# A graph layer on one core: where the third pair's rows, one block of x, one weight and two loads of destinations stand at the hand-over to the edges

## The chip, the core and the metric

One Trainium2 chip; the program runs on one of its cores, in one launch. The metric is the device time of an execution in microseconds (us). Engines are named as in the profile: PE (TensorE matmuls), PEld (its weight loads), DVE (VectorE), ACT (ScalarE), POOL (GpSimd), SP (SyncE, which issues DMAs here); ACTq and SPq are the sequencers of ACT and SP where they issue DMAs.

## The reference

Node features x (6250 x 128), and 100,000 edges (src, dst), sorted by dst. All float32. Cut to what matters:

```python
msg_in   = concatenate([x[src], x[dst]], -1)          # 100000 x 256
h        = relu(msg_in @ Wm1 + bm1)                   # 256
h        = relu(h @ Wm2 + bm2)                        # 256
messages = h @ Wm3 + bm3                              # 128
agg      = segment_sum(messages, dst) / clip(count, 1)
node_in  = concatenate([x, agg], -1)
upd      = relu(node_in @ Wn1 + bn1) @ Wn2 + bn2
out      = layernorm(x + (x + upd))
```

## The kernel before, in words

**Tables.** `x @ Wm1` is computed once a node and not once an edge. Table A (`atab`) holds `x` times the upper half of Wm1, table B (`btab`) `x` times the lower half, split into three bf16 terms. Thirteen blocks of four 128-node tiles are transposed (L307), multiplied (L258) and stored to DRAM by SP (L267 for A, L276 for B). B's rows are put together on their way to DRAM in seven slots of 768 columns (`spare`, `SLOT`, `SLOTS`) in the third plane of `acc`. `acc` is the array of sums, 128 partitions x 3 planes x nodes: two planes are the 256 hidden values, the third counts edges, and the third plane is not summed into until the edges begin. In this stage SP also loads the weights (`weights`, L186), and ACT issues the loads of the edges' destinations for the first three pairs (`destinations`, L375, called at L432; the tiles are `db`, three buffers).

**x's part.** `x_part` (L347) multiplies a block of x by the upper half of Wn1 in two PSUM tiles, adds the bias on ACT or DVE and writes the result over `xT` and `x_sb`. It is four passes of PE a block (two products, each recorded as two passes). Four blocks go between B's last blocks, six behind them (the loop at L447), block 9 (`X_FIRST`) after the first pair's first layer (L687), two more at the end. A small product `pb3` (L449 to L452) gives the bias `b23`.

**Edges.** Edges are taken in groups of 512, and groups in pairs: 98 pairs. For each pair:

- `destinations` loads dst, broadcast over partitions, in two DMAs from ACT (L384);
- `fetch` (L484) gathers A's rows by src with eight indirect DMAs from POOL (L492), and reads B's rows in windows of 22 nodes with eight DMAs (L498). They are SP's, but of the first pair, whose second group's four are ACT's. Both land in `rows`, which has two buffers;
- `hot` (L507) makes on DVE the one-hot matrices that spread B's windows to edges (L516) and edges to nodes (L519);
- `first_layer` (L527) transposes A's rows into PSUM (`ph`, 32 matmuls, L533), adds B's rows by one-hot matmuls (16, L540), and evicts with relu on ACT (four ACTIVATEs, L546). `ph` has one buffer, so the next pair's transposes wait for these evictions;
- `second_layer` (L551) multiplies by Wm2 (32 passes, L555) and evicts on DVE (L557, four);
- `sums` (L559) adds up the edges of a window of nodes (L565), `part_of` copies (L573), `turned` transposes (L584), `add_up` adds the windows into `acc` (L594, DVE).

The steps of neighbouring pairs are interleaved: while pair p is in its first layer, pair p-1 is in its second, p-2 in `sums`, p-3 in `add_up`, and POOL and SP fetch pair p+1. Before the first `add_up`, B's slots in the count plane are cleared on DVE (`clear`, L641): three in step 0, two each after the second layer of steps 1 and 2.

**Order.** The order on PE, ACT and POOL is as written (`manual_schedule`); DVE's is as written from B's last blocks on; SP's is as written while the tables are stored. Each DMA of SP and ACT is given one of eight completion counters in turn, in the program's order, and its issue waits until the DMA that had the counter before has landed. Each engine's queue is in order, so what waits holds up all behind it.

After the edges, the node stage computes the update and the layernorm; the change does not touch it.

Of the kernel before, what the change touches and what calls it, by code (L numbers as in the profile page):

```python
# [9 lines left out]
F32 = mybir.dt.float32  # L10
# [17 lines left out]
def kernel(  # L28
# [121 lines left out]
    with tc.tile_pool(name="prep", bufs=1) as prep, tc.tile_pool(  # L150
# [36 lines left out]
        def weights(block):  # L187
            for t in (wu1, w3, w2):
                nc.vector.tensor_copy(t[:, 0, :1], xT[:, block * 4 * P:block * 4 * P + 1])
            nc.gpsimd.dma_start(nb2[:, 0, :], bm2.rearrange("(o h) -> o h", o=1).to_broadcast([P, H]))  # L190
            nc.sync.dma_start(wu1, wn1.rearrange("(k p) h -> p k h", p=P))
            nc.sync.dma_start(w3, wm3.rearrange("(k p) h -> p k h", p=P))
            nc.sync.dma_start(w2, wm2.rearrange("(k p) h -> p k h", p=P))

# [180 lines left out]
        def destinations(g, ng, dst_row):  # L375

            db = ld.tile([P, 2, 2 * P], I32, name="db", bufs=3)
            if isinstance(g, int) and g < 6:

                nc.vector.tensor_copy(db[:, 0, :1], srcT[:, 0, :1])  # L380
            for h in range(2):
                edges = dst_row[:, ds(g * GE, ng * GE)].rearrange("o (s e) -> o s e", s=ng)
                edges = edges[:, :, h * 2 * P:(h + 1) * 2 * P]
                nc.scalar.dma_start(db[h * NQ:(h + 1) * NQ, :ng, :], edges.to_broadcast([NQ, ng, 2 * P]))  # L384
            return [db[:, k, :] for k in range(ng)]
# [20 lines left out]
        for i in range(BLOCKS):  # L406
# [22 lines left out]
            if i >= BEHIND:  # L429
                b_block(i - BEHIND)  # L430
            if BLOCKS - 3 <= i:
                early.append(destinations(2 * len(early), 2, dst_row))  # L432
        assert not blank
        behind = list(X_BEHIND)
        with tc.manual_schedule(engines={ENG.DVE}):
            for n, j in enumerate(range(BLOCKS - BEHIND, BLOCKS)):
                if n < 4:
                    whole(x_part(behind.pop(0), bank_pb, (nc.scalar, (nc.scalar, nc.vector)[n % 2])))
                b_block(j)
                b_stores()  # L440
            b_terms()
            b_stores()
        stores.close()


        turns.enter_context(tc.manual_schedule(engines={ENG.DVE}))
        for n, b in enumerate(behind):  # L447
            whole(x_part(b, bank_pb, (nc.vector if n >= len(behind) - 2 else nc.scalar, nc.vector)))
        pb3 = pp.tile([P, 1], F32, name="pb3", tag="pp")  # L449
        for c in range(HC):  # L450
            nc.tensor.matmul(pb3, w3[:, c, :], b2[:, c:c + 1], start=(c == 0), stop=(c == HC - 1))
        nc.vector.tensor_add(b23, b3, pb3)  # L452

# [10 lines left out]
    with edge, tc.tile_pool(name="wk", bufs=2) as wk, tc.tile_pool(  # L464
# [18 lines left out]

        def fetch(groups, queues):  # L484


            rows = ld.tile([P, 2, (GT + 1) * H], F32, name="rows", bufs=2)
            got = []
# [37 lines left out]

        def first_layer(got, ohts, nts):  # L527
            ph = p1.tile([P, 2, 2, HC, 2 * P], F32, name="ph")
            for i, ((ag, bw), nt) in enumerate(zip(got, nts)):
                for c in range(HC):  # L530
                    for u in range(GT):
                        for h in range(nt // 2):
                            nc.tensor.matmul(ph[:, i, h, c, u * NQ:(u + 1) * NQ], ag[halves[h], u, c * P:(c + 1) * P],  # L533
                                             ident[halves[h], halves[h]], is_transpose=True,
                                             start=(c == 0 and u == 0), stop=False, skip_group_check=True)
            for i, ((ag, bw), nt) in enumerate(zip(got, nts)):
                for c in range(HC):
# [5 lines left out]
            for i in reversed(range(len(nts))):  # L543
                nh = nts[i] // 2
                for c in range(HC):
                    nc.scalar.activation(h1[:, i, c, :nh * 2 * P].rearrange("p (h e) -> p h e", h=nh),  # L546
                                         ph[:, i, :nh, c, :], AF.Relu, bias=b1[:, c:c + 1])
            return h1
# [89 lines left out]

        slots = list(range(SLOTS))

# [6 lines left out]
        for i in range(NP + 4):  # L647
# [7 lines left out]
            if i < NP:  # L655
                dbs = early.pop(0) if early else destinations(2 * i, min(2, NGF - 2 * i), dst_row)
                if 2 * i + 1 == NGF:
# [3 lines left out]
                          for g, (_, eng) in zip((2 * i, 2 * i + 1), queues)]  # L661
                got = fetch([(srcT[:, 2 * i + k, :], firsts[k]) for k in range(2)], [q for q, _ in queues])
                st[i] = dict(nts=NTS[2 * i:2 * i + 2], got=got, dbs=dbs)
# [17 lines left out]
            if p + 1 < NP:  # L681
                make_hot(p + 1)
            if p == 0:
                clear(3)
            if p < NP:
                s = st[p]
                s["h1"] = first_layer(s.pop("got"), s.pop("ohts"), s["nts"])  # L687
            if p == 0:
                whole(x_part(X_FIRST, bank, (nc.scalar, nc.vector)))
            if 0 <= p - 2 < NP:  # L690
                st[p - 2]["part"] = part_of(summed(p - 2), st[p - 2]["nts"])
            if 0 <= p - 1 < NP:
                s = st[p - 1]
                for j, nt in enumerate(s["nts"]):
# [3 lines left out]
                    second_layer(s["h1"][:, j], h2s[j], nt)  # L698
            if p in (1, 2):
                clear(2)  # L700
        assert not st and not slots
# [260 lines left out]
```

## Time and profile before

| | us |
|---|---|
| median of 4 runs (1144.95 to 1147.65) | 1147.04 |
| the profiled execution: its own time | 1147.92 |
| its span, first to last instruction | 1146.1 |
| outside the span | 1.8 |
| PE busy | 1131.2 |
| POOL busy | 811.4 |
| DVE busy | 682.9 |
| first pair's transposes start (L533) | 75.85 |
| second pair's | 83.96 |
| third pair's | 92.64 |
| fourth pair's | 104.01 |
| fifth pair's | 114.74 |

The profile's page gives busy times by engine, the waits say which engine stood idle for what, the timeline gives instructions in order of time (start, length, what; idle time before it and what ended it in square brackets), and the table by stretches gives busy time and granted TensorE clock between two times. PE's busy time includes matmuls that run at half the clock, so a busy PE is not always a PE at its pace.

### The profile page before, as it was taken

What the parts mean: (1) busy time and instruction counts of PE and PEld (TensorE: products, weight loads), DVE (VectorE), ACT (ScalarE), POOL (GpSimd) and SP (SyncE); (2) the same over time, 40 slices, a digit from 0 to 9 for tenths busy, and PEclk for the clock granted to TensorE, in tenths of its full rate; (3) what the DMA queues carried; (4) which work ended last, traced back from release to release, by engine and by line L of the source; (5) the groups of instructions that cost most, each with busy time, mean ns of one, the idle gap of its engine ahead of it and who ended that gap; (6) DMA issues with size and microseconds to landing.
All of it is one profiled execution on the core that took longest, in us unless ns stands there. A gap on an engine that the chain in (4) does not pass through costs nothing. (4 is left out here: it accounts for less than half of the span.)

```text
span 1146.1 us, 32156 instructions
## 1 busy us (share of the span) xinstructions
PE 1131.2 (99%) x11222; PEld 911.9 (80%) x11223; DVE 682.9 (60%) x2073; ACT 379.4 (33%) x768; POOL 811.4 (71%) x871
## 2 busy tenths in 40 slices
PE   9989999999999999999999999999999999999997
PEld 7757888888888888888888888888888888888566
DVE  5775555555555555565655555555555555555687
ACT  6652333222333322333322233332233332222255
POOL 7867777777777777777777777777777777774222
PEclk9999999999999999999999999999999999999999
DMA  8966666666566666666665656555566555562343
GB/s 260 381 232 184 169 171 172 161 178 179 163 173 172 173 160 179 181 160 172 176 166 162 170 160 161 157 152 160 159 162 162 154 156 157 160 163 74 95 136 101
DMA packets 167754, 193.69 MB, mean 169 GB/s; under 512 B 31074, under 2 KB 133428, under 8 KB 167572
## 3 DMA queue, kind: packets, MB, share of 16 engines
q0 software_dynamic: 38160, 103.75, 33.7%
q1 hardware_dynamic: 100640, 61.84, 18.6%
q10 hardware_dynamic: 28788, 26.01, 7.7%
q8 instruction: 89, 1.46, 0.5%
q14 instruction: 77, 0.63, 0.2%
HBM read 168.97 MB, written 22.88 MB: 167 GB/s over the span
## 5 line engine op out<-in xcount | busy, mean ns | idle before, releaser
L492 POOL DMA_INDIRECT rows<-atab,srcT x784 | 747.9, 954 | 244.3 <-issue 186.8
L555 PE MATMUL bank<-w,h 128*128 128x256 f32 x3128 | 701.3, 382 | 0.7 <-DVE acc L594 0.6
L555 PEld LDWEIGHTS bank<-w,h 128*128 128x128 f32 x3128 | 586.2, 190 | 116.8 <-PE bank L565 40.4
L557 DVE TENSOR_TENSOR h<-bank,nb 128x512 f32<-128x512 f32 x391 | 270.9, 693 | 349.3 <-PE bank L555 327.4
L546 ACT ACTIVATE h<-ph,b 128x512 f32<-128x512 f32 x392 | 237.0, 687 | 694.0 <-PE ph L540 665.7
L594 DVE TENSOR_TENSOR acc<-acc,bank 128x63 f32 x782 | 172.8, 221 | 67.8 <-DVE h L557 34.3
L533 PE MATMUL ph<-ident,rows 64*128 64x64 f32 x3128 | 114.4, 223 | 1.5 <-DMA rows<-atab,srcT 0.9
L533 PEld LDWEIGHTS ph<-ident,rows 64*128 64x128 f32 x3128 | 105.7, 139 | 2.9 <-DMA rows<-atab,srcT 1.1
L565 PE MATMUL bank<-h,oh 128*32 128x257 f32 x1564 | 105.5, 386 | 0.6 <-ACT part L573 0.6
L516 DVE TENSOR_SCALAR oht<-db,pbase 128x128 bf16<-128x128 int32 x392 | 95.7, 296 | 0.6 <-issue 0.2
L573 ACT COPY part<-bank 128x257 f32<-128x257 f32 x196 | 65.5, 402 | 13.7 <-PE bank L565 13.7
L584 PEld LDWEIGHTS bank<-ident,part 64*128 64x128 f32 x1173 | 43.2, 136 | 33.0 <-issue 32.6
L785 POOL TENSOR_TENSOR agg<-total,rc 128x512 f32<-128x512 f32 (+2 forms) x15 | 16.0, 1075 | 68.7 <-DVE total L782 35.4
L540 PE MATMUL ph<-oht,rows 64*128 64x128 bf16 x1564 | 60.7, 217 | 2.8 <-DMA rows<-btab 2.8
L565 PEld LDWEIGHTS bank<-h,oh 128*32 128x32 f32 x1564 | 40.8, 109 | 28.0 <-ACT part L573 1.0
L584 PE MATMUL bank<-ident,part 64*128 64x64 f32 x1173 | 56.7, 229 | 0.3 <-ACT part L573 0.3
L519 DVE TENSOR_TENSOR oh<-iota_n,dloc 128x128 f32<-128x128 f32 x196 | 55.5, 283 | 0.0
L540 PEld LDWEIGHTS <-rows 64*128 64x128 bf16 x1564 | 49.0, 95 | 3.1 <-DMA rows<-btab 3.1
L258 PE MATMUL pbt<-w,xT 128*128 128x256 f32 x196 | 46.6, 382 | 0.3 <-ACT xT L308 0.2
L258 PEld LDWEIGHTS pbt<-w,xT 128*128 128x128 f32 x196 | 35.6, 190 | 7.8 <-DVE rest L285 1.5
L822 PEld LDWEIGHTS pot<-wu,u 128*128 128x128 f32 x192 | 23.6, 192 | 4.8 <-issue 4.3
L795 PE MATMUL put<-agg,wu 128*128 128x512 f32 (+2 forms) x60 | 23.9, 517 | 0.7 <-DVE sh L857 0.4
(134 smaller groups left out, 416.2 us busy)
## 6 DMA issues: line engine op xcount, KB each, us to landing
rows<-btab SPq DMA_DIRECT2D x778, 32.0 KB
db<-in_dst_dram ACTq DMA_DIRECT2D x194, 128.0 KB
rows<-atab,srcT POOLq DMA_INDIRECT x784
btab<-acc SPq DMA_DIRECT2D x24, 384.0 KB
atab<-at SPq DMA_DIRECT2D x24, 256.0 KB
xd<-in_x_dram SPq DMA_DIRECT2D x12, 256.0 KB
x2tab<-xd SPq DMA_DIRECT2D x12, 256.0 KB
x_sb<-in_x_dram SPq DMA_DIRECT2D x5, 512.0 KB
```

Source lines behind the costliest of these rows:

```text
L258: nc.tensor.matmul(pbt[:, a, :], xT[:, (t0 + a) * P:(t0 + a + 1) * P], w1[:, k, :], start=True, stop=True)
L492: nc.gpsimd.indirect_dma_start(out=ag[:, j, :], out_offset=None, in_=atab[:, :], in_offset=bass.IndirectOffsetOnAxis(ap=idx[:, j:j + 1], a ...
L516: nc.vector.tensor_scalar(ohts[:n, i, k, :], db[:n, k * P:(k + 1) * P], pb_cols[:n, k:k + 1], None, op0=ALU.is_equal)
L533: nc.tensor.matmul(ph[:, i, h, c, u * NQ:(u + 1) * NQ], ag[halves[h], u, c * P:(c + 1) * P], ident[halves[h], halves[h]], is_transpose=Tru ...
L540: nc.tensor.matmul(ph[:, i, h, c, k * P:(k + 1) * P], bw[halves[h], k, c * P:(c + 1) * P], ohts[halves[h], i, k, :], start=False, stop=Tru ...
L546: nc.scalar.activation(h1[:, i, c, :nh * 2 * P].rearrange("p (h e) -> p h e", h=nh), ph[:, i, :nh, c, :], AF.Relu, bias=b1[:, c:c + 1])
L555: nc.tensor.matmul(ph2[:, j - j0, :], h1[:, c, j * P:(j + 1) * P], w2[:, c, :], start=(c == 0), stop=(c == HC - 1))
L557: nc.vector.tensor_tensor(h2[:, j0:j0 + 2, :H], ph2, nb2.to_broadcast([P, 2, H]), op=ALU.max)
L565: nc.tensor.matmul(pg[j * WN:(j + 1) * WN, :H + 1], oh[:, j, :], h2[:, j, :], start=True, stop=True, skip_group_check=True)
L573: nc.scalar.copy(part[:nt * WN, i], pg[:nt * WN, :H + 1])
L584: nc.tensor.matmul(pts[h][:, i, c, :], rows, ident[halves[h], halves[h]], is_transpose=True, start=True, stop=True, skip_group_check=True)
L594: nc.vector.tensor_add(window, window, pts[h][:, i, :, k:k + WB])
```

## The change

Five things are moved; no matmul, gather or eviction is added or left out.

- **Third pair's rows.** `fetch` takes a place for its rows. The third pair (i == 2) gets `free_rows`, 2560 columns of the count plane from slot 3 on; all other pairs use the two `rows` buffers as before. Slots are cleared from 0 upwards: three in step 0 and the last four in step 2, behind the third pair's first layer.
- **x's ninth block.** `x_part(X_FIRST)` stands between the transposes and the one-hot matmuls of the first pair. Both its evictions are DVE's (before: one ACT's). Of the first pair's four relu evictions, the first group's two are DVE's now and the second group's two remain ACT's.
- **w2.** Its load, 256 KB, leaves `weights` and is issued by SP behind the last store of B. The one-column copy that held it back is dropped.
- **Destinations.** Those of the first pair alone are loaded during the tables. The second pair's two loads are issued by ACT behind the six x blocks, ahead of ACT's reads of B; the third pair's are issued in the loop, where every later pair's are.
- **pb3** stands before the third of the six x blocks and not after the sixth.

The diff, cut to its core:

```diff
         def weights(block):
-            for t in (wu1, w3, w2):
+            for t in (wu1, w3):
                 nc.vector.tensor_copy(t[:, 0, :1], xT[:, block * 4 * P:block * 4 * P + 1])
...
-            nc.sync.dma_start(w2, wm2.rearrange("(k p) h -> p k h", p=P))
...
             db = ld.tile([P, 2, 2 * P], I32, name="db", bufs=3)
-            if isinstance(g, int) and g < 6:
+            if isinstance(g, int) and g < 2:
...
-            if BLOCKS - 3 <= i:
-                early.append(destinations(2 * len(early), 2, dst_row))
+            if i == BLOCKS - 3:
+                early.append(destinations(0, 2, dst_row))
...
             b_terms()
             b_stores()
+        nc.sync.dma_start(w2, wm2.rearrange("(k p) h -> p k h", p=P))
         stores.close()
...
         for n, b in enumerate(behind):
+            if n == 2:
+                pb3 = pp.tile([P, 1], F32, name="pb3", tag="pp")
+                for c in range(HC):
+                    nc.tensor.matmul(pb3, w3[:, c, :], b2[:, c:c + 1], start=(c == 0), stop=(c == HC - 1))
+                nc.vector.tensor_add(b23, b3, pb3)
             whole(x_part(b, bank_pb, (nc.vector if n >= len(behind) - 2 else nc.scalar, nc.vector)))
-        pb3 = pp.tile([P, 1], F32, name="pb3", tag="pp")
...
-        nc.vector.tensor_add(b23, b3, pb3)
+        early.append(destinations(2, 2, dst_row))
...
-            rows = ld.tile([P, 2, (GT + 1) * H], F32, name="rows", bufs=2)
+        ROWS = (GT + 1) * H
+        FREE = 3
+        free_rows = acc[:, HC, FREE * SLOT:FREE * SLOT + 2 * ROWS].rearrange("p (g r) -> p g r", g=2)
...
+        def fetch(groups, queues, rows=None):
+            if rows is None:
+                rows = ld.tile([P, 2, ROWS], F32, name="rows", bufs=2)
...
-        def first_layer(got, ohts, nts):
+        def first_layer(got, ohts, nts, between=None):
...
+            if between is not None:
+                whole(between)
...
-                    nc.scalar.activation(h1[:, i, c, :nh * 2 * P].rearrange("p (h e) -> p h e", h=nh),
-                                         ph[:, i, :nh, c, :], AF.Relu, bias=b1[:, c:c + 1])
+                    to = h1[:, i, c, :nh * 2 * P].rearrange("p (h e) -> p h e", h=nh)
+                    if between is not None and i == 0:
+                        nc.vector.tensor_scalar(to, ph[:, i, :nh, c, :], b1[:, c:c + 1], 0.0,
+                                                op0=ALU.add, op1=ALU.max)
+                    else:
+                        nc.scalar.activation(to, ph[:, i, :nh, c, :], AF.Relu, bias=b1[:, c:c + 1])
...
-        slots = list(range(SLOTS))
+        slots = list(range(SLOTS))[::-1]
...
-                got = fetch([(srcT[:, 2 * i + k, :], firsts[k]) for k in range(2)], [q for q, _ in queues])
+                got = fetch([(srcT[:, 2 * i + k, :], firsts[k]) for k in range(2)], [q for q, _ in queues],
+                            free_rows if i == 2 else None)
...
-            if p == 0:
-                clear(3)
             if p < NP:
                 s = st[p]
-                s["h1"] = first_layer(s.pop("got"), s.pop("ohts"), s["nts"])
-            if p == 0:
-                whole(x_part(X_FIRST, bank, (nc.scalar, nc.vector)))
+                between = x_part(X_FIRST, bank, (nc.vector, nc.vector)) if p == 0 else None
+                s["h1"] = first_layer(s.pop("got"), s.pop("ohts"), s["nts"], between)
+            if p in (0, 2):
+                clear(FREE if p == 0 else SLOTS - FREE)
...
-            if p in (1, 2):
-                clear(2)
```

More of the change, by code (lines that the diff above doesn't have):

```diff
@@ L447 @@
         for n, b in enumerate(behind):
+            if n == 2:
[3 more added lines that the diff above has]
+                nc.vector.tensor_add(b23, b3, pb3)
             whole(x_part(b, bank_pb, (nc.vector if n >= len(behind) - 2 else nc.scalar, nc.vector)))
-        pb3 = pp.tile([P, 1], F32, name="pb3", tag="pp")
-        for c in range(HC):
-            nc.tensor.matmul(pb3, w3[:, c, :], b2[:, c:c + 1], start=(c == 0), stop=(c == HC - 1))
-        nc.vector.tensor_add(b23, b3, pb3)
+        early.append(destinations(2, 2, dst_row))
     late = ctx.enter_context(tc.tile_pool(name="late", bufs=1))
@@ L482, in flat_bank @@
             return bank().rearrange("p t h -> p (t h)")
-        def fetch(groups, queues):
-            rows = ld.tile([P, 2, (GT + 1) * H], F32, name="rows", bufs=2)
+        ROWS = (GT + 1) * H
+        FREE = 3
+        free_rows = acc[:, HC, FREE * SLOT:FREE * SLOT + 2 * ROWS].rearrange("p (g r) -> p g r", g=2)
+        assert FREE * SLOT + 2 * ROWS <= SLOTS * SLOT
+        def fetch(groups, queues, rows=None):
+            if rows is None:
+                rows = ld.tile([P, 2, ROWS], F32, name="rows", bufs=2)
             got = []
```

## The prediction

> **What bounds the kernel now.** I read the page's busy times first, then PE's waits, then PE's timeline where the tables hand over to the edges, then the queues there.
>
> ```profile
> PE 1131.2 (99%) x11222; PEld 911.9 (80%) x11223; DVE 682.9 (60%) x2073; ACT 379.4 (33%) x768; POOL 811.4 (71%) x871
> ```
>
> PE is the bound, and the change removes none of its work. Only PE's idle and slow time can move. Its waits:
>
> ```profile
> PE ph L540 <- DMA rows<-btab: 2.8, 2, 2.3
> ...
> PE ph L533 <- DMA rows<-atab,srcT: 0.9, 1, 0.9
> ...
> PE bank L555 <- DVE acc L594: 0.6, 1, 0.6
> PE ph L533 <- DVE b L452: 0.6, 1, 0.6
> ```
>
> All four lie in one place. PE's timeline there:
>
> ```profile
> 74.78 0.50 PE L451 MATMUL pb<-b,w 128*128 128x1 f32 x4
> 75.85 1.21 PE L533 MATMUL ph<-ident,rows 64*128 64x64 f32 x32 [0.57 <-DVE b L452]
> 76.89 0.22 PE L540 MATMUL ph<-oht,rows 64*128 64x128 bf16 x1
> 79.38 0.23 PE L540 MATMUL ph<-oht,rows 64*128 64x128 bf16 x2 [2.27 <-DMA rows<-btab]
> 80.10 0.92 PE L540 MATMUL ph<-oht,rows 64*128 64x128 bf16 x13 [0.48 <-DMA rows<-btab]
> 80.95 3.07 PE L355 MATMUL bank<-xT,wu 128*128 128x512 f32 x4
> 83.96 1.21 PE L533 MATMUL ph<-ident,rows 64*128 64x64 f32 x32
> ...
> 94.59 0.52 PE L533 MATMUL ph<-ident,rows 64*128 64x64 f32 x10 [0.95 <-DMA rows<-atab,srcT]
> ...
> 107.25 1.10 PE L555 MATMUL bank<-w,h 128*128 128x256 f32 x4 [0.63 <-DVE acc L594]
> ```
>
> The starts of transposes (L533), 75.85, 83.96, 92.64, 104.01, 114.74, are 8.11, 8.68, 11.37 and 10.73 apart; from then on a pair takes 10.06. So what the change can reach is about 6 us. Some of it is slow clock, in the table by stretches (us; busy time of PE, PEld, DVE, ACT, POOL; granted clock; DMA share and GB/s):
>
> ```profile
> 76.36:79.77 3.41, 0.98 (x27) 0.67 (x21) 3.19 (x14) 0.00 (x0) 0.02 (x1) 1.00 0.47 125
> 79.77:83.18 3.41, 3.08 (x16) 1.83 (x17) 1.12 (x2) 2.07 (x4) 1.58 (x2) 0.50 0.21 55
> ```
>
> After 3.41 us in which PE was busy for 0.98, the clock is 0.50 for 3.41 us: block 9's four passes (L355) take 3.07 where the 24 before them took 10.46, 1.74 for four. Last, the queues (ACT, POOL, and a wait of SP):
>
> ```profile
> 73.94 2.52 ACTq L498 DMA_DIRECT2D rows<-btab  x4
> 81.30 0.94 POOL L492 DMA_INDIRECT rows<-atab,srcT  x1 [4.92 <-DMA rows<-btab]
> SPq L267 <- DMA db<-in_dst_dram: 0.6, 1, 0.6
> ```
>
> ACT's four reads of B go out without a wait; POOL stands 4.92 us for a `rows` buffer; and a store of A waited for a load of destinations with which it shares nothing but a completion counter, so these waits bind.
>
> **The change, part by part.**
>
> *Third pair's gathers.* POOL is done with the second pair at 76.4 and need not wait for a buffer: the place in the count plane is free once B's last store has landed, before 73.94, when the reads of B start. The eight gathers take 10.0 us (81.30 to 91.28), so the last goes out at 85.5 and not at 90.04. PE's wait ended at 94.59, 4.55 after that issue; now the data are there at 90.0, ahead of 92.6. The pair's transposes and one-hot matmuls took 2.85 us (92.64 to 95.49) where the fourth pair's took 1.54: **-1.31**.
>
> *Clearing.* Two clears (1.50 us, at 104.50) stood between the last L557 and the first `add_up`, and PE waited at 107.25. They move ahead of those L557s, where four of 0.77 (three take 2.31) have room: the fourth pair takes 10.06 and not 10.73: **-0.67**. Were the room gone, L557 would come up to 3.1 us late on four PSUM banks 1.72 us apart: no stall below some 3 us, one for one above.
>
> *pb3.* Its 0.43 us of PE move ahead of the last x eviction, which so ends at 76.2 in place of 75.73; the first transposes start at 76.25, 0.4 later. The wait for B's rows covers that.
>
> *Block 9.* Its 1.74 us fit between 77.3 and 79.1, before B's rows land (79.38): nothing, where it cost 3.07. But it also covered the relu evictions: ACT's four took 2.42 beside it. Now two on ACT (1.27) and two on DVE (0.75 each, as L360; 1.45 with overlap) stand bare between the first pair's last matmul and the second's transposes: 1.65 with two hand-offs of 0.1.
>
> *B's rows.* The moved issues themselves are hidden: w2's 0.55 us on SP falls between the last store's issue at 69.0 and 73.94, the second pair's two of 0.6 on ACT between its last x eviction at 71.4 and 73.94, both idle there. I leave the start of the reads at 73.94: the DMA share was 0.98 to 0.99 from 63 to 72, the stores follow DVE, and the loads taken out earlier lie before idle DMA time at 57 to 63. Bounds: 0.3 earlier (a gather's share) to 1.3 later (w2 and the second pair's destinations are 512 KB behind or beside the last store, at some 390 GB/s). SP's four reads go out at 73.94 to 76.3 as before; the last landed at 80.1, 3.8 after its issue, where a read at 82.44 in a quiet time took 2.3. ACT's four are new. In the built order of the changed kernel the first waits for w2's landing, the second for the second pair's destinations, the third for SP's second read, the fourth for SP's fourth: they have each other's counters. What queues behind is ACT alone: two evictions that need these rows anyway. SP's fourth lands between 78.6 (2.3 after issue) and 80.1; I take 79.4, for ACT's reads now compete less. ACT's fourth then goes out at 79.5 and lands 2.3 to 3.8 later; I take 2.4, for only gathers run beside it: 81.9. Five matmuls follow (0.3), then the evictions (1.65): the second pair's transposes start at 83.85, where they started at 83.96: **-0.1** (bounds 82.0 to 86.0).
>
> *Clock.* From 79.1 until 83.85 PE has about 0.9 us of work, fewer than 0.98 in 3.41. So I expect another 3.41 us at half clock. It fell on block 9 before; now 2.8 us of it fall on the second pair's first layer and the first's second: **+1.4** (0 to 1.7).
>
> [...]
>
> *Third pair's destinations.* They were there from the start. Now ACT issues them behind the first pair's evictions, the second half behind the landing of SP's second read of the third pair: 84.1 plus 2.3, 86.4. A load issued at 90.74 landed at 94.3, so here 89.9. DVE stands at the third pair's one-hots until then; six instructions (1.3) and four L557 (0.65 each, back to back) end at 94.0. PE needs the last of them for the second group's sums at 83.85 + 1.4 + 1.6 + 7.1 + 2.0 = 96.0: covered by 2 us. ACT, held by the same counter until 87.0, owes its next evictions from about 86.9 on. With a PE 3 us earlier it would cost 1.
>
> Sum: -1.31 - 0.67 - 0.1 + 1.4 = **-0.7**, so 1147.92 becomes 1147.2. The profiled execution lies 0.88 above the median of the runs; the forecast in the median's terms is **1146.3**. All else, from the fifth pair to the end, is PE at its pace and stays.
>
> **The rivals.**
>
> *Faster.* ACT's reads land with SP's at 80.1: first layer done at 80.4, transposes at 82.05, -1.9; the clock then stays full, since PE is idle for little over 2 us. With -1.98 this is -3.9; the late destinations give back 1.1 (L557 done at 94.0, wanted at 92.9): -2.8, 1144.2, and 1143.1 if they land by 88.7. For it: each wait is bounded by a landing that could be 2 us. Against: the fourth read cannot go out before SP's fourth lands.
>
> *Slower.* One mechanism: the counters chain two slow landings. SP's fourth at 80.1, ACT's fourth 3.8 later, 84.0; transposes at 85.95, +2.0; the clock's half window whole, +1.7; less 1.98: +1.7, and 1148.7; with the reads of B 1.3 later +3.0, 1150.0. It decides from a last landing at about 82.6, 0.7 past mine.
>
> *The change does nothing there.* The gathers come early but second-layer evictions wait for destinations that land 4 us later than I think (94): the sums wait 2, the -1.98 is gone, 1148.3. Against it: the load at 90.74 took 3.5.
>
> **How the numbers follow.** About 2.3 us, 0.2%, is what a measurement of this kernel can tell from no change. The likeliest case (-0.7, its own range 1144.6 to 1148.4): 0.44. Faster: 0.35, nearly all beyond 0.2%, for my landings in a crowded stretch err easily by 1.5 us, and two of the three gains have direct rows. Slower: 0.15, most beyond 0.2%. Destinations: 0.06. So faster 0.36, same 0.48, slower 0.16. Leaving a tenth out at each end, the range is 1143.0 to 1149.3.
>
> **What the changed profile would show.** Gathers without a gap at 76.4 and no wait for them before the third pair; the fourth pair 10.06 long; ACTq's reads of B spread from about 75 to 80 and not 2.52 us together; block 9 at 0.43 a pass; PE idle around 80 to 84; a stretch of clock 0.50 some 3 us later than before. It would prove me wrong if ACT's last read landed before 80.5, if the clock stayed at 1.00, or if PE waited in the sums for L557.

## The result, and the profile after

The changed kernel takes 1149.36 us (median of 38 runs, 1147.52 to 1156.23), the kernel before 1146.87 beside it (58 runs, 1144.13 to 1149.37). The ratio is 1.0023 with a 95% interval of [1.0018, 1.0028]: slower by 2.1 to 3.2 us. The forecast was 1146.3, in a range that ended at 1149.3.

The profiled execution spans 1148.0 us (before: 1146.1). PE's waits around the hand-over (engine, tile and line; what was waited for: us in total, times, longest):

```profile
PE ph L540 <- DVE h L557: 3.1, 1, 3.1
PE ph L549 <- DMA rows<-btab: 2.4, 3, 1.0
PE ph L540 <- DVE xT L359: 0.8, 1, 0.8
```

The two waits of before that the change was to shorten, for `rows<-atab` and for `acc`, are gone. The wait for B's rows is still there, and a new one stands at the top: PE waits 3.1 us for DVE's evictions, where the forecast had 1.65 for them. The same stretch in PE's timeline (start, us, engine, line, operation, tiles, count, idle before and what ended it):

```profile
76.35 1.21 PE L540 MATMUL ph<-ident,rows 64*128 64x64 f32 x32 [0.84 <-DVE xT L359]
77.49 1.98 PE L354 MATMUL bank<-xT,wu 128*128 128x512 f32 x4
79.41 0.23 PE L549 MATMUL ph<-oht,rows 64*128 64x128 bf16 x1
...
82.98 0.34 PE L549 MATMUL ph<-oht,rows 64*128 64x128 bf16 x5 [1.00 <-DMA rows<-btab]
86.37 1.97 PE L540 MATMUL ph<-ident,rows 64*128 64x64 f32 x32 [3.05 <-DVE h L557]
88.10 1.09 PE L549 MATMUL ph<-oht,rows 64*128 64x128 bf16 x16
...
96.93 1.22 PE L540 MATMUL ph<-ident,acc 64*128 64x64 f32 x32
...
107.06 1.16 PE L540 MATMUL ph<-ident,rows 64*128 64x64 f32 x32
```

The starts of transposes (L540 here, L533 before; the fifth at 117.11) are 10.02, 10.56, 10.13 and 10.05 apart; they were 8.11, 8.68, 11.37 and 10.73. The last two steps have gained what was forecast, 1.24 and 0.68. The first two have lost more, 1.91 and 1.88: the last of B's rows comes at 82.98, and between the first pair's last one-hot matmul and the second pair's transposes PE is idle for 3.05 us. ACT and DVE in that stretch (two timelines, ACT first; `ACTq` is ACT's issue of DMAs):

```profile
75.14 6.17 ACTq L505 DMA_DIRECT2D rows<-btab  x4
83.40 1.27 ACT L560 ACTIVATE h<-ph,b 128x512 f32<-128x512 f32 x2 [11.46 <-DMA rows<-btab]
```

```profile
84.70 1.41 DVE L557 TENSOR_SCALAR h<-ph,b 128x512 f32<-128x512 f32 x2 [4.44 <-ACT h L560]
...
91.67 0.48 DVE L523 TENSOR_SCALAR oht<-db,pbase 128x128 bf16<-128x128 int32 x2 [3.14 <-DMA db<-in_dst_dram]
```

ACT's four reads of B are issued over 6.17 us; before they took 2.52. DVE's two evictions start only when ACT's two have ended. And the clock, in stretches cut where it changes (us; busy time of PE, PEld, DVE, ACT, POOL; granted clock; DMA share, GB/s):

```profile
80.35:83.77 3.42, 1.14 (x15) 0.53 (x15) 0.00 (x0) 0.37 (x1) 2.52 (x3) 1.00 0.55 153
83.77:87.18 3.41, 0.81 (x16) 0.84 (x17) 2.26 (x4) 0.90 (x2) 2.50 (x4) 0.50 0.51 146
87.18:90.59 3.41, 3.41 (x42) 2.94 (x40) 1.24 (x2) 1.36 (x3) 2.55 (x3) 0.50 0.85 206
```

It stands at half for 6.83 us, twice as long as before. The second of the two windows is full of work, all of it slow.

### The profile page after: what moved, and what is told of

It reads as the page before. It is cut to its first block, busy times and chain, and to the rows that moved or that the text cites. A ratio compares the mean times of both kernels' runs of the same rounds, so it can differ in the third digit from the quotient of the medians.

```text
span 1148.0 us, 32151 instructions
## 1 busy us (share of the span) xinstructions
PE 1132.0 (99%) x11222; PEld 912.6 (79%) x11223; DVE 684.3 (60%) x2073; ACT 377.9 (33%) x765; POOL 810.4 (71%) x871
## 5 line engine op out<-in xcount | busy, mean ns | idle before, releaser
L499 POOL DMA_INDIRECT rows<-atab,srcT x776 | 739.3, 953 | 240.4 <-issue 185.7
L560 ACT ACTIVATE h<-ph,b 128x512 f32<-128x512 f32 x390 | 235.9, 687 | 697.4 <-PE ph L549 678.9
L540 PE MATMUL ph<-ident,rows 64*128 64x64 f32 x3096 | 113.4, 223 | 3.9 <-DVE h L557 3.1
L540 PEld LDWEIGHTS ph<-ident,rows 64*128 64x128 f32 x3096 | 105.0, 140 | 4.9 <-issue 3.2
```

The lines of the kernel that those rows point to most:

```text
L499: nc.gpsimd.indirect_dma_start(out=ag[:, j, :], out_offset=None, in_=atab[:, :], in_offset=bass.IndirectOffsetOnAxis(ap=idx[:, j:j + 1], a ...
L560: nc.scalar.activation(to, ph[:, i, :nh, c, :], AF.Relu, bias=b1[:, c:c + 1])
```

## The experiments

The 58 runs of the kernel before lie up to 5 us apart, so beside the ratio I read one stretch of each profile: from the start of the last table matmul (`pbt`) to the start of the fifth pair's transposes, with everything the change touches inside. Outside it little differs: the last table matmul starts 0.12 us later after the change, and the fifth pair to the end takes 1030.85 us in place of 1031.40. Times in the table are us from the last table matmul, each from one profiled execution: until PE's last wait for the first pair's rows of B has ended ("at most" where PE did not wait for them: the start of the first one-hot matmul that needs the last of the rows), until the second pair's transposes, until the fifth's; then how long the clock was at half in the stretch.

| kernel | rows there | second pair | fifth pair | half clock | ratio to before |
|---|---|---|---|---|---|
| before | 15.84 | 19.70 | 50.48 | 3.4 | |
| changed | 18.60 | 21.99 | 52.73 | 6.8 | 1.0023 [1.0018, 1.0028] |
| rows and clearing alone | 15.50 | 18.95 | 49.36 | 3.4 | 0.9997 [0.9984, 1.001] |
| block 9 and pb3 alone | at most 15.3 | 19.61 | 50.65 | 3.4 | 1.0017 [1.0007, 1.0028] |
| late loads alone | 18.65 | 22.79 | 53.22 | 10.2 | 1.0009 [1.0001, 1.0018] |
| changed, two PSUM tiles | 18.51 | 18.63 (first half) | 50.21 | 3.4 | 1.0001 [0.9992, 1.001] |
| changed, destinations back | 16.51 | 20.12 | 50.46 | 3.4 | 1.0002 [0.9993, 1.0011] |
| changed, w2 back | 17.23 | 20.62 | 52.05 | 6.8 | 1.0014 [1.0005, 1.0023] |
| rows, clearing, block 9 | at most 15.3 | 18.71 | 50.33 | 6.8 | 1.0007 [0.9998, 1.0017] |
| the same, two PSUM tiles | at most 15.3 | 17.31 | 49.64 | 3.4 | 0.9999 [0.9983, 1.0014] |
| changed, PE filled | 17.96 | 21.38 | 51.04 | 0 | 1.0016 [1.0007, 1.0025] |
| rows and clearing, PE filled | 16.92 | 20.04 | 50.82 | 0 | 1.0006 [0.9997, 1.0015] |
| rows, block 9, two tiles, filled | 17.29 | 19.18 | 50.94 | 3.4 | 1.0005 [0.9996, 1.0014] |
| all eased | 16.38 | 18.27 | 48.31 | 0 | 0.9985 [0.9976, 0.9994] |

**The parts alone.** First the third pair's gathers and the clearing, on the kernel before:

```diff
-        slots = list(range(SLOTS))
+        slots = list(range(SLOTS))[::-1]
...
+                            free_rows if i == 2 else None)
...
-            if p == 0:
-                clear(3)
...
+            if p in (0, 2):
+                clear(FREE if p == 0 else SLOTS - FREE)
...
-            if p in (1, 2):
-                clear(2)
```

> One part alone: the third pair's gathered rows in the count plane and the clears moved with them; block 9, pb3, w2 and the destinations stand as before. Theory (this part is sound and the loss comes from the others): POOL has no gap at 76.4, the third pair takes 10.1 us and not 11.4, the fourth 10.06 and not 10.73, so -1.9 us against the kernel before (ratio 0.9983). Rival (POOL's gathers, now running while B's rows are read, delay those reads): PE's first one-hot matmuls end after 81.0, a us or more is given back, ratio 0.9992 or above.

The stretch is 1.12 us shorter. The steps from the third and from the fourth pair gained 0.86 and 0.62, together 0.5 less than the forecast 1.98. Of the two steps before them the first gained 0.74 and the second lost 1.11: block 9 still ran at half clock (3.03 us), the second pair's transposes now did too (1.72 us and not 1.21), and PE waited 0.36 for that pair's rows of B. The whole run can't be told from before: the theory's 0.9983 lies just outside the interval. The rival's reason didn't show, since the first pair's rows were there 0.34 us sooner than before. Then block 9 and pb3 by themselves:

```diff
-                s["h1"] = first_layer(s.pop("got"), s.pop("ohts"), s["nts"])
-            if p == 0:
-                whole(x_part(X_FIRST, bank, (nc.scalar, nc.vector)))
+                between = x_part(X_FIRST, bank, (nc.vector, nc.vector)) if p == 0 else None
+                s["h1"] = first_layer(s.pop("got"), s.pop("ohts"), s["nts"], between)
```

> One part alone: block 9 inside the first first layer with the relu evictions split over DVE and ACT, and pb3 early; the rows, clears, w2 and destinations stand as before. Theory (block 9 had covered the relu evictions, and DVE's two stand behind ACT's two): reads of B land at 80.1 as before, the last matmul of the first layer at 80.5, then 2.8 us of bare evictions, the second pair's transposes at 83.3 (-0.6); the clock is halved after that for about 1.5 us of loss, and the third pair's wait for gathers falls away with it (-1.3): between -1 and +0.5 us, ratio 0.9991 to 1.0004. Rival (the filled wait is a gain): second pair's transposes at 82.1, clock full, -1.9 us or more, ratio below 0.9985.

Block 9 lies in the wait, as forecast: B's rows are all there when it ends. But nothing now covers the evictions. PE's timeline of this kernel:

```profile
79.36 0.62 PE L548 MATMUL ph<-oht,rows 64*128 64x128 bf16 x16
83.95 1.96 PE L539 MATMUL ph<-ident,rows 64*128 64x64 f32 x32 [3.97 <-DVE oht L522]
```

PE is idle for 3.97 us (the profile names the instruction behind DVE's evictions, which run from 82.29 to 83.69; here DVE's three clears, still in their old place, come before them too), and the half clock after it falls on the second pair (its transposes take 1.96 us, 1.21 at full clock). So this part alone gains nothing and loses 0.1% to 0.3%, which is worse than either expectation. Third, the loads:

```diff
-            for t in (wu1, w3, w2):
+            for t in (wu1, w3):
...
-            if BLOCKS - 3 <= i:
-                early.append(destinations(2 * len(early), 2, dst_row))
+            if i == BLOCKS - 3:
+                early.append(destinations(0, 2, dst_row))
...
+        nc.sync.dma_start(w2, wm2.rearrange("(k p) h -> p k h", p=P))
...
+        early.append(destinations(2, 2, dst_row))
```

> One part alone: w2 and the second and third pair's destinations loaded late; rows, clears, block 9 and pb3 stand as before. Theory (the loads' completion counters chain ACT's four reads of B): ACT's reads spread from 75.1 to 80.8, the last lands at about 83, the second pair's transposes start 2.3 us later than before: +2 to +3 us, ratio 1.0017 to 1.0026. Rival (the late loads are harmless, the loss is block 9's): ratio 0.9995 to 1.0005, reads of B together as before.

In the stretch this is the costliest part: 2.74 us more. In whole runs it is 1.0009, below the theory's 1.0017 (the interval just reaches it), and not to be told from block 9's loss. ACT's reads of B, then the clock:

```profile
73.93 6.54 ACTq L504 DMA_DIRECT2D rows<-btab  x4
```

```profile
74.75:78.16 3.41, 1.21 (x32) 1.07 (x32) 1.71 (x11) 0.00 (x0) 0.00 (x0) 1.00 0.68 152
78.16:81.57 3.41, 1.22 (x11) 0.55 (x11) 3.08 (x9) 0.00 (x0) 0.00 (x0) 0.50 0.22 59
81.57:84.99 3.42, 2.87 (x10) 1.41 (x9) 0.18 (x1) 2.23 (x4) 1.62 (x2) 0.50 0.25 64
```

The reads are spread as in the changed kernel, with none of its other parts present. The DMA share is 0.68 and then 0.22 while they are, so it is no lack of bandwidth that spreads them. Three windows go at half clock; the third begins at 84.99.

**Which wait spreads the reads.** In the changed kernel either load may do it, by its traffic or by its counter. First the destinations go back to the tables:

```diff
-            if i == BLOCKS - 3:
-                early.append(destinations(0, 2, dst_row))
+            if BLOCKS - 3 <= i:
+                early.append(destinations(2 * len(early), 2, dst_row))
...
-        early.append(destinations(2, 2, dst_row))
```

> The changed kernel with the two destination loads issued during the tables again; w2 stays late, and the rest of the change stays. In its built order ACT's first three reads of B wait for no other landing, and the fourth for w2's alone. Theory (the chain of completion counters delays the rows, and it hangs on the destinations): ACT's four reads go out together, within 3 us, the last lands 1.5 to 3 us sooner, and the stretch from the last table matmul to the fifth pair's transposes, 52.73 us in the changed kernel, becomes 50.0 to 51.2; the time falls by 1.5 to 2.7 us against the changed kernel. Rival (the reads land late because loads put behind the tables fill the queues, and the counters do not matter): w2 still lands beside the reads, the last landing moves by less than 0.7 us, and the stretch stays above 52.0.

ACT's queue in this kernel:

```profile
74.09 2.51 ACTq L504 DMA_DIRECT2D rows<-btab  x4
```

All four go out together, the rows are there 2.1 us sooner (16.51 for 18.60), and the stretch is 2.27 us shorter: the theory's numbers. w2 is still loaded late, and held up none of the four. SP's fourth read landed where it did in the changed kernel (16.5 us after the last table matmul in both); but there ACT's fourth waited for it, and here it didn't. Then w2 goes back and the destinations stay late:

```diff
-            for t in (wu1, w3):
+            for t in (wu1, w3, w2):
...
+            nc.sync.dma_start(w2, wm2.rearrange("(k p) h -> p k h", p=P))
...
-        nc.sync.dma_start(w2, wm2.rearrange("(k p) h -> p k h", p=P))
```

> The changed kernel with w2 loaded among the other weights again; the destinations stay late. In its built order ACT's first read of B waits for the stores alone, but the second still waits for the second pair's destinations and the third and fourth for SP's second and fourth reads. Theory (the chain hangs on the destinations and on SP's reads): only the first read moves, about 1 us earlier, the last landing moves by 0 to 0.7 us, and the stretch of 52.73 us becomes 52.0 to 52.8. Rival (w2 is the first link, so all links move up with it): the last landing moves up by 1 us or more and the stretch is 51.5 or less.

```profile
73.82 5.16 ACTq L505 DMA_DIRECT2D rows<-btab  x4
```

Here the two theories share the result. The first read goes out 9.75 us after the last table matmul in place of 10.76, the issue of the last ends 14.91 after it in place of 16.93, and the rows are there 1.37 us earlier, as the rival had it. But the stretch is 52.05, which is the theory's number: again two windows went at half clock. Nor was it w2's link that brought the rows sooner. In the changed kernel ACT's second, third and fourth reads went out so:

```profile
77.18 0.50 ACTq L505 DMA_DIRECT2D rows<-btab  x1
78.21 0.48 ACTq L505 DMA_DIRECT2D rows<-btab  x1
80.83 0.48 ACTq L505 DMA_DIRECT2D rows<-btab  x1
```

Though the first had waited for w2, the third was out by 78.69; then ACT stood 2.1 us for SP's fourth (at 80.85 PE goes on with the matmul that needs that one's row). With w2 back the fourth waits for SP's fourth just so, but that landed 2.3 us after its issue, and 4.5 after it in the changed kernel. SP's fourth took between 2.3 and 5.2 us over all executions in which its landing shows. So the link that decides is the last one: in the five kernels with the second pair's destinations late, the rows are there 2.1 to 3.2 us after ACT's fourth read, which goes out when SP's fourth has landed; in the other nine PE waits for no row behind SP's fourth. Over the thirteen kernels with a change the rows are there 18.0 to 18.7 us after the last table matmul in the four with the whole chain, 17.2 with w2 back, and from at most 15.3 to 17.3 in the eight with the destinations where they were. The spread of the last group is as large as the link.

**The evictions.** The first layer's sums get two PSUM tiles, one for each group:

```diff
-            ph = p1.tile([P, 2, 2, HC, 2 * P], F32, name="ph")
+            ph = [p1.tile([P, 2, HC, 2 * P], F32, name=f"ph_{i}") for i in range(2)]
```

> The changed kernel with the first layer's PSUM tile in two, one for each group, so that DVE's relu evictions need not stand behind ACT's. Theory (3.05 us of PE's idle time before the second pair are these evictions in a row): the first group's are done before ACT's last read lands, the second pair's transposes start about 0.1 us after the first pair's last matmul, 3 us earlier than in the changed kernel; the clock is still halved for about 3.4 us behind the idle time from 79.6 on: -2.5 to -3.2 us against the changed kernel, ratio against before 0.9996 to 1.0002. Rival (the evictions are not what PE waits for): within 0.5 us of the changed kernel, ratio 1.0019 to 1.0025.

In the changed kernel with two tiles, DVE evicts the first group as soon as SP's reads of B are in, and PE starts the second pair's first half at once (DVE's timeline, then PE's):

```profile
79.09 1.40 DVE L557 TENSOR_SCALAR h<-ph,b 128x512 f32<-128x512 f32 x2
```

```profile
81.79 0.34 PE L549 MATMUL ph<-oht,rows 64*128 64x128 bf16 x5 [0.81 <-DMA rows<-btab]
81.91 0.71 PE L540 MATMUL ph<-ident,rows 64*128 64x64 f32 x16
83.53 0.93 PE L540 MATMUL ph<-ident,rows 64*128 64x64 f32 x16 [0.91 <-ACT h L560]
```

The wait of 3.05 became one of 0.91, with B's rows as late as in the changed kernel (18.51); the stretch is 2.52 us shorter, and half clock lasted for one window and not two (3.41 us, from 83.83). So DVE's evictions stood behind ACT's because both read one tile, and not for want of data or of an engine: with two tiles DVE's run from 79.09 and ACT's from 82.21.

**Rows, clearing and block 9 together, loads where they were.** The changed kernel with both loads put back (the two diffs above):

> The change without its late loads: third pair's gathers, clearing, pb3 and block 9 as in the changed kernel, w2 and all destinations loaded where they were. Theory (the parts add: rows and clearing alone 49.36 us in the stretch from the last table matmul to the fifth pair's transposes, block 9 alone 50.65, before 50.48; the late loads are what costs): 48.6 to 50.0, and a time 0.5 to 2 us below the kernel before. Rival (block 9 and the early gathers collide, since DVE's evictions wait for ACT's and the gathers compete with the reads of B): 50.5 or more, and no gain over the kernel before.

```profile
83.17 1.97 PE L539 MATMUL ph<-ident,rows 64*128 64x64 f32 x32 [3.05 <-DVE h L556]
```

```profile
78.91:82.32 3.41, 1.21 (x18) 0.45 (x16) 2.21 (x4) 1.26 (x2) 2.76 (x3) 1.00 0.53 151
82.32:85.73 3.41, 2.56 (x48) 2.59 (x48) 3.08 (x8) 0.00 (x0) 2.54 (x3) 0.50 0.49 136
85.73:89.15 3.42, 3.42 (x14) 2.60 (x9) 0.67 (x4) 2.42 (x4) 2.51 (x4) 0.50 0.50 149
```

PE waits for no row of B at all, has the same 3.05 us of evictions, and then two windows at half clock. 50.33 is above the 48.6 to 50.0 that the theory gave; the rival came nearer (its bound was 50.5). The late loads cost 52.73 - 50.33 = 2.4 us, block 9 and pb3 on top of the early gathers 50.33 - 49.36 = 1.0, and the gathers and clearing bring 1.1: together the +2.25 of the changed kernel (single executions, differenced one from the next, so the sum comes out by itself). In whole runs either repair alone, two tiles (1.0001) or the destinations (1.0002), took the changed kernel's loss away, and neither brought a gain. With two tiles on top:

> The run before it in this list, and the first layer's sums in two PSUM tiles, one for each group, so that DVE's two evictions of the first pair wait for no eviction of ACT's. Theory (evictions in a row cost 1.4 us of PE's wait): the stretch is 1.0 to 2.0 us shorter than without the two tiles, 47 to 48.8, and the time 2 to 4 us below the kernel before. Rival (PE is then released sooner into half clock, which takes it back): less than 0.7 us shorter than without the two tiles.

```profile
82.74 1.21 PE L539 MATMUL ph<-ident,rows 64*128 64x64 f32 x32 [1.65 <-issue]
83.75 0.57 PE L548 MATMUL ph<-oht,rows 64*128 64x128 bf16 x9
85.43 0.69 PE L548 MATMUL ph<-oht,rows 64*128 64x128 bf16 x7 [1.10 <-DMA rows<-btab]
```

The evictions now run side by side (ACT's from 81.17, DVE's from 81.23) and cost 1.65, the prediction's own figure for two on ACT beside two on DVE. But the stretch gains 0.69 and not 1.0 to 2.0, which is the rival's number: PE now comes too early for the second pair's rows, waits 1.10 there, and the clock still falls to half (0.50 from 85.09 to 88.50).

**The clock.** Two extra matmuls of w_u1 with x, four passes in 1.98 us, which nobody reads, go behind block 9 and two more behind the one-hots:

```diff
+        def fill(n):
+            to = flat_bank() if n else None
+            for _ in range(n):
+                nc.tensor.matmul(to, wu1[:, 0, :P], xT[:, :4 * P], start=True, stop=True)
...
             if between is not None:
                 whole(between)
+            fill(extra[0])
...
+            fill(extra[1])
             h1 = wk.tile([P, 2, HC, GE], F32, name="h1")
```

> The changed kernel with extra matmuls in PE's two idle places at the first pair: two of w_u1 with x (four passes, 1.74 us) behind block 9, before the one-hots, and two more behind the one-hots, before the second pair's transposes. Nobody reads what they write; they end before PE has anything else to do. Theory (a window of 3.41 us with too little work of PE halves the clock of the next: in ten profiles every window with 1.6 us or less did, none with 2.1 or more): the clock stays 1.00, the second pair's transposes and first layer take 1.8 us in place of 2.9, the step from the second to the third pair's transposes 8.6 to 8.9 us in place of 10.56, and the stretch from the last table matmul to the fifth pair's transposes 50.5 to 51.5 in place of 52.73. Rival (half clock takes nothing, because late destinations or rows hold the second pair anyway): the clock is full but the step stays above 10 and the stretch above 52.2.

PE's timeline of the changed kernel so filled:

```profile
81.82 1.98 PE L537 MATMUL bank<-xT,wu 128*128 128x512 f32 x4
84.97 1.21 PE L545 MATMUL ph<-ident,rows 64*128 64x64 f32 x32 [1.17 <-DVE h L564]
...
93.66 1.22 PE L545 MATMUL ph<-ident,acc 64*128 64x64 f32 x32
```

The clock is full throughout (1.00 in every stretch from 69.5 to 93.3). The step from the second to the third pair's transposes takes 8.69 us in place of 10.56, and the stretch 51.04 in place of 52.73: the theory's numbers, from work that computes nothing. The next step gives 0.72 back (10.85 for 10.13), and the rows of B were there 0.64 sooner here. In whole runs the difference to the changed kernel is smaller and its interval overlaps. The same filling (two matmuls, before the one-hots) in the kernel with rows and clearing alone:

> Third pair's gathers and clearing alone, and two extra matmuls (1.74 us, read by nobody) between the first pair's transposes and its one-hots, where PE waits for B's rows; block 9 stays behind the one-hots. Theory (clock by windows): full clock throughout, block 9 and what follows 1.5 us shorter, of which the evictions, now covered by block 9 for 1.74 us alone, take 0.6 to 1.0 back: the stretch 48.2 to 49.0 in place of 49.36. Rival (nothing: what half clock cost was hidden by the evictions): 49.2 or more.

A miss: the clock is full (1.00 from 69.5 to 93.3) and the stretch is 50.82, longer than without. PE's waits there, then DVE:

```profile
PE ph L553 <- DMA rows<-btab: 1.8, 2, 1.7
PE bank L602 <- DVE h L575: 1.6, 2, 1.2
```

```profile
98.51 0.48 DVE L521 TENSOR_SCALAR oht<-db,pbase 128x128 bf16<-128x128 int32 x2 [5.12 <-DMA db<-in_dst_dram]
...
99.89 3.12 DVE L662 MEMSET acc<- 128x768 f32 x4
102.93 2.42 DVE L575 TENSOR_TENSOR h<-bank,nb 128x512 f32<-128x512 f32 x4
```

Two things take the gain back. B's rows came 1.4 us later than in the run without filling. And with PE earlier, DVE is late: it stands until 98.51 for the fourth pair's destinations, then makes four clears, then the third pair's second-layer evictions, for which PE waits 1.6 us. Filling the kernel with block 9 in the wait and two tiles (one matmul behind the one-hots, one before the second pair's):

> Third pair's gathers, clearing, block 9 in the wait, loads where they were, two PSUM tiles, and one extra matmul (0.87 us, read by nobody) behind the first pair's one-hots and one between the second pair's transposes and its one-hots. Theory (clock by windows): no half clock, the stretch 47.5 to 48.4 in place of 49.64, the time 2 to 3 us below the kernel before. Rival (the second pair's rows, for which PE waited 1.1 us, hold it and the clock's loss was beside that wait): 49.2 or more.

A miss too. B's rows came 17.29 us after the last table matmul, where the run without filling had them by 15.3; PE was idle 1.98 us ahead of them, with no filling in that place, and the clock fell to half for 3.4 us. The last kernel fills there also and makes the four clears ahead of the fourth pair's one-hots:

```diff
-            if p + 1 < NP:
+            if p + 1 < NP and p != 2:
                 make_hot(p + 1)
...
                 clear(FREE if p == 0 else SLOTS - FREE)
+            if p == 2:
+                make_hot(p + 1)
```

> Third pair's gathers, clearing, pb3 and block 9 as in the changed kernel, loads where they were, two PSUM tiles, and one extra matmul (0.87 us, read by nobody) at each of three places: before and behind the first pair's one-hots, and between the second pair's transposes and its one-hots. Further, DVE makes the last four clears ahead of the fourth pair's one-hot matrices and not behind them, since it stood until 98.5 us for that pair's destinations and the clears and the third pair's second-layer evictions came after. Theory (the front is bound by B's rows, the clock and then these destinations, and all three are now eased): no half clock, no wait of PE for evictions in the sums, the stretch from the last table matmul to the fifth pair's transposes 47.0 to 49.0 us, the time 1.5 to 3 us below the kernel before. Rival (B's rows decide, and they land between 15 and 17 us after the last table matmul from one execution to the next): 49.5 or more, and no gain over the kernel before.

```profile
81.72 0.56 PE L554 MATMUL ph<-oht,rows 64*128 64x128 bf16 x13 [0.21 <-issue]
82.21 1.12 PE L536 MATMUL bank<-xT,wu 128*128 128x512 f32 x2
83.61 1.21 PE L544 MATMUL ph<-ident,rows 64*128 64x64 f32 x32 [0.27 <-PE bank L536]
...
93.46 1.22 PE L544 MATMUL ph<-ident,acc 64*128 64x64 f32 x32
...
103.59 1.16 PE L544 MATMUL ph<-ident,rows 64*128 64x64 f32 x32
```

```profile
94.39 3.12 DVE L663 MEMSET acc<- 128x768 f32 x4
98.46 0.48 DVE L522 TENSOR_SCALAR oht<-db,pbase 128x128 bf16<-128x128 int32 x2 [0.95 <-DMA db<-in_dst_dram]
```

No half clock (1.00 from 72.8 to 89.8), no wait in the sums, steps of 6.30, 9.85, 10.13 and 10.05, and 48.31 in the stretch. The time is 1145.93 us (11 runs) beside 1147.62 for the kernel before: 0.9985 [0.9976, 0.9994]. It is the only kernel here that the measurement puts ahead of the one before. It still does 3.3 us of matmuls for nothing; useful work in their place wasn't tried.

## Why the prediction was wrong

*Third pair's gathers (-1.31) and clearing (-0.67).* Right: the steps gained 1.24 and 0.68 in the changed kernel, and there is no gap on POOL at 76.4.

*pb3 and block 9.* Right in their own terms: the first transposes came 0.38 later against the last table matmul (forecast 0.4) and were covered, and block 9 fit the wait at full clock. What it left uncovered is the next term.

*The evictions, 1.65 bare.* This term failed first: 3.05 us. I had priced two evictions on ACT beside two on DVE, each with its own row, and had not asked whether they may run side by side. Both read `ph`, one tile, and in the built order DVE's first waits for ACT's second. The trace says so in one line (DVE L557 <- ACT h L560), the run with two tiles showed 0.91, and the one with early loads and two tiles showed the 1.65 itself.

*B's rows, last landing at 81.9.* The second term: with the last table matmul at the same place, 64.26 against 64.38, they came at 82.98. The chain was read rightly, link by link; its sizes were not. The one that failed is SP's fourth landing: I took 79.4, 3.1 us after its issue, with 80.1 as the late end; ACT's fourth read, which waits for it, went out at 80.83. It then landed in 2.1 us, a little faster than the 2.4 assumed. The first link, w2's landing, came late too (ACT's first read went out at 75.14, and I had let it start at 73.94), but did not decide. Against the last table matmul the rows are 0.96 later than forecast, the evictions 1.40 longer: the second pair's transposes moved by +2.29 and not by -0.1. Why SP's fourth read took 4.5 us from its issue, at 76.30, stays open.

*Clock, +1.4.* Right in kind, 1.88 measured, since two windows went at half and not one. The forecast went by the row of before (0.98 us of PE work in 3.41, then clock 0.50), and the runs bear that out better than the longest gap: in the kernel with early loads and two tiles no gap in the stretch was above 1.65 us, and behind 3.42 us with 1.59 us of PE work the clock was 0.50 all the same. That it stays full with PE idle for little over 2 us, as *Faster* had it, was not shown: in the changed kernel with two tiles PE was idle for 2.06 of 3.42 us (80.41 to 83.83), and the clock after them was 0.50.

*Third pair's destinations, covered by 2 us.* They landed at 91.7 and not 89.9, and PE, itself later than forecast, did not wait in the sums: covered. Whether they would have been with PE on time was not shown.

The sum was -0.7; measured in the stretch it is 2.29 + 1.88 - 1.24 - 0.68 = +2.25. Evictions (1.40), rows (0.96) and clock (0.48) make up 2.84 of the 2.95 between. Of the rivals *Slower* came nearest: it had the chain of landings, and 1149.36 lies between its two figures, 1148.7 and 1150.0. That is partly luck: it had the last landing at 84.0 or later and the evictions at 1.65, while the landing came at 82.98, and the serial evictions, in no case of mine, made up for it.

## What to carry to other kernels

When work that covered something is moved, look for what it covered: block 9 filled PE's wait for B's rows and thereby uncovered the evictions, for which PE then stood idle for 3.05 us. Before pricing two engines side by side, see whether they touch one tile: here the program made the second wait for the first, and two tiles undid it (PE's wait 3.05 us, then 0.91). And see which completion counters a moved load leaves to what is issued behind it: here, with two loads moved for the sake of an earlier stage, ACT's fourth read came to wait for SP's fourth, and the rows were there 2.1 to 3.2 us after that one.

## What the runs showed of the hardware

Half clock lasted 3.41 us in the profile before, 6.83 in the changed kernel's and 10.24 with late loads alone (78.16 to 88.40). In the stretch it did not go by the longest gap: that was 1.65 us in the kernel with early loads and two tiles, where the clock fell, and 1.65 in the filled one with rows and clearing, where it did not. In these rows it went with PE's busy time in the 3.41 us at full clock ahead of it:

| kernel | stretch, at clock 1.00 | PE busy, us | clock in the next 3.41 us |
|---|---|---|---|
| before | 76.36:79.77 | 0.98 | 0.50 |
| changed | 80.35:83.77 | 1.14 | 0.50 |
| late loads alone | 74.75:78.16 | 1.21 | 0.50 |
| rows, clearing, block 9 | 78.91:82.32 | 1.21 | 0.50 |
| changed, two PSUM tiles | 80.41:83.83 | 1.36 | 0.50 |
| rows, clearing, block 9, two tiles | 81.67:85.09 | 1.59 | 0.50 |
| rows and clearing, PE filled | 78.97:82.38 | 1.83 | 1.00 |
| changed, two PSUM tiles | 77.00:80.41 | 2.16 | 1.00 |
| changed, PE filled | 82.32:85.74 | 2.25 | 1.00 |

The one with 1.83, and what came after it:

```profile
78.97:82.38 3.41, 1.83 (x18) 1.12 (x19) 0.00 (x0) 0.96 (x2) 2.79 (x3) 1.00 0.55 152
82.38:85.80 3.42, 2.77 (x52) 1.83 (x51) 2.15 (x3) 2.25 (x5) 2.52 (x3) 1.00 0.51 141
```

The rows do not make a rule for the whole execution: at the end of the kernel with block 9 alone, in the 3.41 us from 1138.73, PE was busy for 1.51 us, and the clock after it stayed at 1.00. At half clock as much PE work did not bring the full clock back: 3.41 us with 0.81 (changed), 1.22 and 2.87 (late loads) or 2.56 us of it (rows, clearing, block 9) were followed by 0.50, those with 3.07 (below), 3.08 (before) or 3.41 (changed) by 1.00. A window that led into half clock and the one that led out of it, from the kernel with early loads and two tiles:

```profile
81.67:85.09 3.42, 1.59 (x41) 1.38 (x41) 3.09 (x7) 0.77 (x2) 2.51 (x4) 1.00 0.55 152
85.09:88.50 3.41, 3.07 (x13) 2.34 (x14) 1.03 (x6) 2.34 (x4) 2.75 (x3) 0.50 0.54 155
```

Where half clock falls in the hand-over differs from one profile to the next: it first starts at 78.16 us with late loads alone, at 79.77 before, at 83.77 in the changed kernel and at 85.09 in the one above; and the same longest gap, 1.65 us, cost a window in one kernel and none in another. With the 2.0 us or more by which B's rows came earlier or later in kernels whose loads stand where they did (at most 15.3 to 17.29 us after the last table matmul), I estimate that this is enough to hide a part worth 1 us in whole runs; that it is the only reason was not shown.
